# A four-layer image model on one core: eight PSUM banks for the first front, and a planner that lays parts of a front side by side

## The chip, the cores and the metric

The kernel runs on one core of a Trainium2 chip. Its time is the device time of one execution in microseconds, given as the median of several runs. All data are fp32. PE is TensorE, DVE is VectorE, ACT is ScalarE, POOL is GpSimd and SP is SyncE, which issues most DMAs here.

## The reference

Eight images of 56 x 56 tokens with 192 channels go through four layers. Each layer normalizes its input in groups and adds its output to its input:

```python
x = x + _L0_conv_ref(_gn(x), ...)   # gated Toeplitz mixing along rows and columns
x = x + _L1_conv_ref(_gn(x), ...)   # shifted 7x7 window attention, 6 heads
x = x + _L2_conv_ref(_gn(x), ...)   # depthwise 3x3 convolution
x = x + _L3_conv_ref(_gn(x), ...)   # selective scan in 4 directions, 384 channels, 16 states
```

Layer 0 is `p * (o1 + o2)` with an output projection; p, q and v are `silu(x @ w.T + b)`, and o1 and o2 are Toeplitz products of q * v along the two axes. Layer 1 is softmax attention in windows of 49 tokens with a bias table and a mask. Layer 3 projects to two halves (one becomes the gate z), convolves 3x3, and then for each direction and channel runs

```python
delta = softplus(delta + delta_bias)
h[t] = exp(delta[t] * A) * h[t - 1] + delta[t] * u[t] * B[t]     # 16 states n
y[t] = sum over n of h[t] * C[t]  (+ D * u[t])
```

The four directions are summed, normalized over channels, multiplied with silu(z) and projected.

## The kernel before

**Setup.** The kernel first makes the Toeplitz coefficients, then q * v for all images (L188 to L220), then the Toeplitz products for all images (L228 to L277), then small constants.

**Front and loop.** Everything else is organized by image. `front(b)` prepares image b for the scan and consists of five stages: `gate` (the rest of layer 0), `attention` (layer 1), `conv2` (layer 2), `inner` (projection and 3x3 convolution of layer 3, for three blocks of 128 channels) and `steps` (delta, B and C, for 14 chunks). All stages carve their buffers out of one SBUF tile, `slab`. The scan itself is a loop over `pairs`: 8 images x 4 directions (`slot`) x 7 chunks of 448 tokens x 3 channel blocks `d` x 8 pairs of states `k`, that is 672 pairs for an image and 24 for a chunk. `finish(b, j)` is the end of layer 3 for one chunk.

**One pair** of the loop is, with its lines: `inject` on POOL (hs <- du, bm, L989), `decay` on ACT (two exponentials into PSUM, ps_a, L1004), `scan` on DVE (L1013), `times_c` on DVE for five of eight k and on POOL for k = 1, 4, 6 (hc, L1019), small copies of states on ACT (L994, L1026), and `add_up` on PE (eight 64-row matmuls of hc with the identity into ps_y, L1036). The tile hc has four buffers. After the eight pairs of a d, `sums` copies ps_y to SBUF on ACT (ysb, L1047, which takes one of the same four buffers), folds it on PE (L1052) and adds it to ysum on DVE (L1056, L1061). B and C of a chunk (bm, cm) are loaded by SP one chunk ahead.

**Banks.** PSUM has eight banks: ps_a takes four (two buffers of two), ps_y two and the pool `ps` two. `bank()` takes one of the two in `ps`. Fronts, `sums` and `finish` share them.

**What sets the order.** Image 0's front is drained by itself before the loop: `drain(front(0), costs.setdefault("front", []))` runs the generator to its end, and the order of its instructions on each engine is left to the framework's scheduler. This also records a cost for each engine and step, by a formula for each instruction (`Meter`); the profile puts these instructions on line L76. The loop is written in an order of its own (`manual_schedule`), and every engine executes in this order. While pair g of image b is issued, `Parts.step(limit)` may put in steps of front(b + 1), `sums` and `finish`. A generator yields `held, needs`: how many banks it now holds, and how many its next step takes. The planner keeps a model time for each engine. `fits` lets in a step if by the recorded costs it would end on ACT before a limit, on PE by 5 us after the next scan's start (`n1 + 5.0`), and on DVE without a wait over 0.2 us. A refused step gets 3 us more each time (`grace`). A part that has just taken a bank is not resumed in the same step; at most two banks are held in all. DMAs have no cost in the model, so a yield after a load says nothing of when the data will be there.

At the last chunk of an image the next front must be complete. What is left of it is then put in without a limit:

```python
if i + 1 in range(4 * NCH, len(chunks), 4 * NCH):
    while fronts[b + 1] in parts.clients:
        parts.step(anything)
```

Of the kernel before, what the change touches and what calls it, by code (L numbers as in the profile page):

```python
# [81 lines left out]
def model(ctx: ExitStack, tc: tile.TileContext, a: dict, out: bass.AP):  # L82
# [197 lines left out]
    with (  # L280
# [3 lines left out]
        tc.tile_pool(name="ps_a", bufs=2, space=PSUM) as psa,  # L284
        tc.tile_pool(name="ps_y", bufs=1, space=PSUM) as psy,
        tc.tile_pool(name="ps", bufs=2, space=PSUM) as ps,
# [82 lines left out]

        st = wp.tile([CP, 2, NCH, 6], F32, name="gn_st")  # L370
# [49 lines left out]
        def gate(b):  # L420
# [26 lines left out]
            yield 0, 0  # L447
            yield from absorb(w_p, stats0[:, b], p_b, nb[:CP, :6], CP, 6)
            for j in range(NCH):
# [3 lines left out]
                for c in range(6):  # L453
                    yield 0, 1
                    p = bank()
                    for k in range(2):
                        nc.tensor.matmul(
                            p[:CP, :CH], w_p[:, k, c * CP : (c + 1) * CP], x[:, j % 2, k, :], start=k == 0, stop=k == 1
                        )
                    yield 1, 0  # L460
                    nc.scalar.activation(s[:, c, :], p[:CP, :CH], AF.Identity, bias=nb[:CP, c : c + 1])
                yield 0, 0
                nc.scalar.activation(s, s, AF.Silu)
                usual_functions()
                for c in range(6):
# [3 lines left out]
                    yield 0, 1  # L469
# [13 lines left out]
                for m in range(2):  # L483
# [10 lines left out]
                    nc.vector.bn_stats(out=st[:, m, j, :], in_=xm)  # L494
                nc.sync.dma_start(out=blocks(x1_d[b])[:, :, tok], in_=x[:, j % 2])
# [3 lines left out]
        def attention(b):  # L499
# [36 lines left out]
            yield 0, 0  # L536
# [15 lines left out]
            for wh in range(H // WS):  # L552
# [10 lines left out]
                for m in range(4):  # L563
# [13 lines left out]
                    )  # L577
                if wh + 1 < H // WS:
                    load_x(wh + 1)
                for q in range(4):  # L580
# [52 lines left out]
                    for g in range(2):  # L633
# [9 lines left out]
                        )  # L643
                    yield 0, 1
# [13 lines left out]
                for m in range(2):  # L658
# [12 lines left out]
                    for cd, cs in ((slice(0, W - SHIFT), slice(SHIFT, W)), (slice(W - SHIFT, W), slice(0, SHIFT))):  # L671
                        nc.vector.scalar_tensor_tensor(
                            x[:, m, :, cs], pi[:, :, cd], vb[:, m : m + 1], x[:, m, :, cs], ALU.add, ALU.add
                        )
                for i0, i1, h0 in rows(wh):
# [4 lines left out]
        def conv2(b):  # L680
# [17 lines left out]

            for j in range(NCH):
                nc.sync.dma_start(out=xo[:, j % 2], in_=blocks(x2_d[b])[:, :, j * CH : (j + 1) * CH])  # L700
                yield 0, 0
                for k in range(2):
                    nc.vector.bn_stats(out=st[:, k, j, :], in_=xo[:, j % 2, k, :])
            load_x(0)
# [49 lines left out]
        def inner(b):  # L754
# [4 lines left out]
            for d in range(ND):  # L759
# [8 lines left out]
                yield 0, 0  # L768
# [3 lines left out]
                for j in range(NCH):  # L772
                    if j + 1 < NCH:
                        load_x(j + 1)
                    for u in range(2):
                        yield 0, 1
                        p = bank()
                        for k in range(2):
                            nc.tensor.matmul(
                                p[:, :CH], w_in[:, k, u * 128 : (u + 1) * 128], x[:, j % 2, k, :], start=k == 0, stop=k == 1  # L780
                            )
                        yield 1, 0
                        if u:
                            nc.scalar.activation(zt[:, j % 2, :], p[:, :CH], AF.Identity, bias=nb[:, 1:2])
                            nc.sync.dma_start(out=zr_d[b][:, d, j * CH : (j + 1) * CH], in_=zt[:, j % 2, :])
                        else:
                            nc.scalar.activation(
                                xp[:, 8 * j + 1 : 8 * j + 9, 1 : W + 1],
                                p[:, :CH].rearrange("p (h w) -> p h w", w=W),
                                AF.Identity,  # L790
                                bias=nb[:, 0:1],
                            )
                nc.sync.dma_start(out=dg, in_=dg3_d[:, d])
                yield 0, 0
# [20 lines left out]
                for src, dst in ((xc, xc_d[0][b]), (xT, z_d[b])):  # L815
                    yield 0, 0
# [13 lines left out]
        def steps(b):  # L830
# [10 lines left out]
            yield 0, 0  # L841
            for n, (o, j) in enumerate(todo):
# [10 lines left out]
                for d in range(ND):  # L853
                    yield 0, 2
                    held = []
                    for s in range(2):
                        row = slice(32 * s, 32 * s + R)
                        held.append(bank())
                        nc.tensor.matmul(
                            held[s][:, :CH], w_dt[row, o, d * 128 : (d + 1) * 128], rc[row, n % 2, :], start=True, stop=True  # L860
                        )
                    yield 2, 0
                    for s in range(2):
                        nc.scalar.activation(
                            dl[:, s, d, :], held[s][:, :CH], AF.Identity, bias=dt_b[:, 2 * o + s, d : d + 1]
                        )
                yield 0, 0
# [196 lines left out]
        class Parts:  # L1064
# [4 lines left out]
            def __init__(self):  # L1069
                self.clients = []  # L1070
                self.t = dict.fromkeys("PADE", 0.0)
# [5 lines left out]
            def add(self, work, name, now=False):  # L1077
                entry = Entry(work, costs.setdefault(name, []), now)
                self.clients.insert(0 if name != "front" else len(self.clients), entry)
                return entry  # L1080

            def fits(self, entry, limit):
# [5 lines left out]
                for engine, cost in entry.costs[entry.at]:  # L1088
# [5 lines left out]
            def resume(self, entry):  # L1094
                got = log_of(entry.work, entry.costs) if entry.at == len(entry.costs) else next(entry.work, None)
                at = entry.ready
                for engine, cost in entry.costs[entry.at]:
                    at = self.run(engine, cost, at)
                entry.at += 1
                if got is None:  # L1100
                    self.clients.remove(entry)
                    return
                entry.held, entry.needs = got
                entry.ready = at

            def step(self, limit):
                old = [e for e in self.clients if e.held]
                for entry in old + [e for e in self.clients if e not in old]:
                    while entry in self.clients:
                        if entry.held and entry not in old:  # L1110
# [11 lines left out]
        class Entry:  # L1122
            def __init__(self, work, costs, now):
                self.work, self.costs, self.now = work, costs, now
                self.at = self.held = self.needs = self.waits = 0
                self.ready = 0.0

        def log_of(work, log):

            nonlocal nc  # L1130
            nc, meter.log = meter, []
            got = next(work, None)
            log.append(meter.log)
# [3 lines left out]
        def drain(work, log=None):  # L1137

            while (next(work, None) if log is None else log_of(work, log)) is not None:
                pass  # L1140

        drain(front(0), costs.setdefault("front", []))
        with tc.manual_schedule():
# [29 lines left out]
            fronts = {}  # L1173
            ending, anything = None, dict.fromkeys("ADE", 1e9)
            for g, (i, d, k) in enumerate(pairs):
                b, slot, j = chunks[i]
                if i % (4 * NCH) == 0 and d == 0 and k == 0 and b + 1 < B:
                    fronts[b + 1] = parts.add(front(b + 1), "front")
                more = i + 1 < len(chunks)
# [32 lines left out]
                if k == 2 and g > NP:  # L1212
                    parts.add(sums(*((i, d - 1) if d else (i - 1, ND - 1))), "sums", now=True)
                if slot == 0 and b > 0 and ((j, d, k) == (0, 0, 5) or j + 1 < NCH and (d, k) == (2, 4)):
                    while ending in parts.clients:
                        parts.step(anything)
                    ending = parts.add(finish(b - 1, j + (d == 2)), "finish")

                n1 = max(parts.t["D"], fed[g + 1], set_[g + 1])
                n2 = n1 + (2.02 if on_pool(*pairs[min(g + 1, last)][1:]) else 3.11)  # L1220
                parts.step({"A": max(n2, fed[g + 2]) - 0.7, "E": n1 + 5.0, "D": 0.2})
# [111 lines left out]
```

## Time and profile before

| | |
|---|---|
| median of 3 runs (lowest to highest) | 23384.04 us (23373.92 to 23392.59) |
| the profiled execution's own time | 23375.31 us |
| its span in the profile | 23373.5 us |
| setup, until the first load of gate(0) is used | to 2487 us |
| front of image 0 by itself | 2487 to 3863 us |
| first scan of images 1 to 7 | 6250, 8733, 11217, 13690, 16167, 18646, 21133 us |
| last scan ends, then the end of layer 3 | 23164 us, 23373 us |
| PE, DVE, ACT, POOL busy | 17477, 16533, 13090, 16164 us |

The page gives busy times, then 40 slices of the span with busy tenths; a stretch of time can be asked for with the busy time of each engine in it; the list of waits puts the idle time ahead of an instruction down to the instruction or DMA that ended it; the timeline has single instructions in order of time. An instruction is named by its line, what it writes and what it reads (`hc<-ps_a,cm`). [...]

### The profile page before, as it was taken

How to read it: one execution, taken by the hardware profiler on the slowest of the kernel's cores; microseconds unless marked ns; L12 is line 12 of the kernel's file. 1: busy time of each engine (PE TensorE's matmuls, PEld its weight loads, DVE VectorE, ACT ScalarE, POOL GpSimd, SP SyncE). 2: the span in 40 equal slices, each digit the busy share in tenths (PEclk: the TensorE clock that was granted, in tenths of full speed). 3: DMA queues.
4: the chain of work that ended last, by engine and by line, in shares of the span. 5: the costliest groups of instructions: out<-in, count | busy, mean ns of one | idle time of the engine just before them, and what ended most of it. 6: DMA issues, size and time to landing. Idle time of an engine off the chain costs nothing. (4 is left out here: it accounts for less than half of the span.)

```text
span 23373.5 us, 251077 instructions
## 1 busy us (share of the span) xinstructions
PE 17477.1 (75%) x82852; PEld 7258.6 (31%) x82852; DVE 16533.0 (71%) x13158; ACT 13089.9 (56%) x32542; POOL 16163.7 (69%) x8500
## 2 busy tenths in 40 slices
PE   8866677778787778777877777787877787775555
PEld 4566333322232223222332233222322232222112
DVE  3211113887788868887788778877887788878996
ACT  3211224665767565756665666656675667565554
POOL 0000003887888778877888778877887788778997
PEclk9987777778787879687877887787878786877667
DMA  3487214434553455345543554345534554454432
GB/s 89 113 194 169 65 53 148 138 118 151 174 149 112 143 178 151 116 133 172 164 126 115 168 168 134 116 146 179 143 119 143 176 150 124 126 175 138 129 122 89
DMA packets 2536537, 3223.64 MB, mean 138 GB/s; under 512 B 1045261, under 2 KB 2488687, under 8 KB 2504272
## 3 DMA queue, kind: packets, MB, share of 16 engines
q1 hardware_dynamic: 2515010, 3091.32, 44.9%
q0 software_dynamic: 15520, 116.14, 1.3%
q8 instruction: 657, 10.76, 0.2%
q14 instruction: 646, 5.29, 0.1%
q10 hardware_dynamic: 4704, 0.12, 0.0%
HBM read 2631.56 MB, written 575.48 MB: 137 GB/s over the span
## 5 line engine op out<-in xcount | busy, mean ns | idle before, releaser
L989 POOL TENSOR_TENSOR hs<-du,bm 128x896 f32<-128x896 f32 x5376 | 11111.6, 2094 | 147.8 <-DVE ps_a L1013 134.5
L1013 DVE TENSOR_TENSOR_SCAN ps_a<-ps_a,hs 128x898 f32<-128x898 f32 x3360 | 6783.1, 2019 | 876.6 <-ACT ps_a L1004 704.9
L1036 PE MATMUL ps_y<-hc,ident_sb 64*64 64x448 f32 x43008 | 6628.7, 714 | 924.9 <-POOL hc L1019 901.5
L1004 ACT ACTIVATE ps_a<-delta,A_logs_sb 128x449 f32<-128x449 f32 x10752 | 6859.6, 638 | 348.8 <-DVE hs L1013 67.7
L1019 POOL TENSOR_TENSOR hc<-hs,cm 128x896 f32<-128x896 f32 x2016 | 4049.3, 2009 | 2961.8 <-DVE hs L1013 1613.2
L1019 DVE TENSOR_TENSOR hc<-ps_a,cm 128x896 f32<-128x896 f32 x3360 | 3668.1, 1092 | 1604.7 <-PE ps_y L1036 654.5
L1013 DVE TENSOR_TENSOR_SCAN hs<-ps_a,hs 128x898 f32<-128x898 f32 x2016 | 4066.1, 2017 | 356.9 <-ACT ps_a L1004 327.6
L1036 PEld LDWEIGHTS ps_y<-hc,ident_sb 64*64 64x64 f32 x43008 | 1466.3, 162 | 4500.0 <-issue 2667.5
L1026 ACT COPY state<-ps_a 128x2 f32<-128x2 f32 x3359 | 535.6, 159 | 3542.9 <-DVE hc L1019 3536.5
L977 POOL TENSOR_TENSOR du<-delta,xcd 128x448 f32<-128x448 f32 x672 | 712.9, 1061 | 1319.3 <-DMA xcd<-xc 1319.3
L1052 PE MATMUL ps_f<-ysb,fold 128*64 128x448 f32 x2684 | 919.1, 774 | 704.9 <-ACT ysb L1047 564.9
L800 PE MATMUL ps_f<-slab 128*128 128x448 f32 x2646 | 1153.5, 573 | 118.2 <-DMA slab<-dg_d 108.9
L263 PE MATMUL ps_tz<-tzx,tm 112*112 112x112 f32 x4608 | 889.4, 369 | 469.6 <-issue 306.1
L277 POOL DMA_DIRECT2D o<-tzx x192 | 98.0, 514 | 1496.9 <-DVE tzx L269 1010.6
L263 PEld LDWEIGHTS ps_tz<-tzx,tm 112*112 112x112 f32 x4608 | 884.0, 200 | 475.3 <-issue 474.2
L269 DVE COPY tzx<-ps_tz 112x448 f32<-112x448 f32 x288 | 179.9, 625 | 1178.4 <-PE ps_tz L263 866.9
L1047 ACT COPY ysb<-ps_y 128x896 f32<-128x896 f32 x671 | 605.0, 902 | 572.7 <-PE ps_y L1036 571.3
L1026 ACT COPY state<-hs 128x2 f32<-128x2 f32 x2016 | 381.2, 189 | 940.8 <-DVE hs L1013 908.1
L732 PE MATMUL ps_f<-slab 96*96 96x448 f32 x1764 | 785.5, 583 | 105.0 <-DVE slab L719 94.0
L76 PE MATMUL ps_f<-slab 96*96 96x448 f32 (+6 forms) x2306 | 780.8, 520 | 92.4 <-DMA slab<-x 29.2
L269 ACT COPY tzx<-ps_tz 112x448 f32<-112x448 f32 x288 | 153.3, 532 | 1204.2 <-PE ps_tz L263 947.7
L994 ACT COPY hs<-state 128x2 f32<-128x2 f32 x4608 | 817.6, 177 | 3.5 <-POOL hc L1019 3.1
(223 smaller groups left out, 19723.7 us busy)
## 6 DMA issues: line engine op xcount, KB each, us to landing
bm<-bc SPq DMA_DIRECT2D x1792, 448.0 KB
cm<-bc SPq DMA_DIRECT2D x1792, 448.0 KB
xcd<-xc SPq DMA_DIRECT2D x840, 224.0 KB
dl<-slab SPq DMA_DIRECT2D x224, 672.0 KB
delta<-dl SPq DMA_DIRECT2D x224, 672.0 KB
tzx<-qv SPq DMA_DIRECT2D x192, 588.0 KB
o<-tzx POOLq DMA_DIRECT2D x192, 588.0 KB, 16.3
slab<-x SPq DMA_DIRECT2D x224, 336.0 KB
```

The source lines that it names most:

```text
L76: return f(*args, **kw)
L263: nc.tensor.matmul(po[:, c, :], t[:, c2 + c, :], x[:, :, c1 + c2 + c], start=True, stop=True)
L732: nc.tensor.matmul(p[:CP, :CH], dg[:, k, t, :], xp[:, u, k, dy : dy + 8, dx : dx + W], start=t == 0, stop=t == 8,)
L800: nc.tensor.matmul(p[:, :CH], dg[:, t, :], xp[:, 8 * j + dy : 8 * j + dy + 8, dx : dx + W], start=t == 0, stop=t == 8,)
L989: nc.gpsimd.tensor_mul(hs[:, :, tokens(i)[0]], dus[i, d].to_broadcast([128, NG, CH]), bms[i, k])
L994: nc.scalar.copy(hss[g][:, :, tokens(i)[1]], src)
L1004: nc.scalar.activation(dA[:, n, :], deltas[i][:, d, at : at + CH + 1], AF.Exp, scale=negA[:, slot, d, c : c + 1])
L1013: nc.vector.tensor_tensor_scan(h, dA, hs, 0.0, ALU.mult, ALU.add)
L1019: (nc.gpsimd if on_pool(d, k) else nc.vector).tensor_mul(hc, h[:, :, tokens(i)[0]], cms[i, k])
L1026: nc.scalar.copy(states[i][:, d, NG * k : NG * k + NG], h[:, :, tokens(i)[2]])
L1036: nc.tensor.matmul(yps[i, d][64 * n : 64 * n + 64, r, :CH], ident[row, row], hcs[g][row, n, :], start=k == 0, stop=k == NP - 1,)
L1052: nc.tensor.matmul(pf[64 * r : 64 * r + 64, :CH], fold, sb[:, r, :], start=True, stop=True)
```

## The change

**Banks for image 0.** The three PSUM pools are no longer opened at the top. `front(0)` is drained with a pool `ps` of eight banks, and the loop's pools (ps_a, ps_y, ps with two) are opened after it.

**Parts side by side.** A generator may now yield a list of generators. Each becomes an `Entry` of its own whose parent waits until all are done; `later` keeps their steps in the order of the list. In the front these are the six gates, the six gated products and the two outputs of `gate`, the four queries, two transposes and two outputs of `attention`, the 14 projections of `inner`, and the six deltas of `steps`. The latter took two banks at a time before and now take one each. `drain` runs up to six of a list in turn. In `gated` and `projected` the load of the next block moves behind the yield, into the step that fills the bank.

**Transfer times.** A yield may carry a third number, which is added to the time at which the planner takes the next step's inputs to be ready: 6 us after a stage's first loads, 5 before Silu in `inner`, 8 in `steps`. In `conv2` the statistics now load two blocks ahead, with a step for each `bn_stats`.

**Pace and limits.** `parts.work` sums the costs of the front's steps. `parts.late` is set while that share is behind the share of the image's pairs plus 24. While it is set, a part that has just taken a bank may go on in the same step. The limit on PE is 1.5 us in place of 5 for k = 0 and 1. `sums` gets the time at which its last add ends as its ready time.

```diff
-        tc.tile_pool(name="ps_a", bufs=2, space=PSUM) as psa,
-        tc.tile_pool(name="ps_y", bufs=1, space=PSUM) as psy,
-        tc.tile_pool(name="ps", bufs=2, space=PSUM) as ps,
...
             load_x(0)
             load_ot(0)
-            yield 0, 0
+            yield 0, 0, 6.0
...
-                for c in range(6):
+
+                def gates(c):
                     yield 0, 1
                     p = bank()
...
                     yield 1, 0
                     nc.scalar.activation(s[:, c, :], p[:CP, :CH], AF.Identity, bias=nb[:CP, c : c + 1])
-                yield 0, 0
+
+                yield [gates(c) for c in range(6)]
                 nc.scalar.activation(s, s, AF.Silu)
                 usual_functions()
-                for c in range(6):
+
+                def gated(c):
+                    yield 0, 1
                     n = 3 * j + c // 2
                     if c % 2 == 0 and n + 1 < 3 * NCH:
                         load_ot(n + 1)
-                    yield 0, 1
...
+                yield [gated(c) for c in range(6)]
+                yield [output(m) for m in range(2)]
...
+            def load_all(j):
+                nc.sync.dma_start(out=xo[:, j % 2], in_=blocks(x2_d[b])[:, :, j * CH : (j + 1) * CH])
+
+            load_all(0)
+            load_all(1)
+            yield 0, 0, 6.0
             for j in range(NCH):
-                nc.sync.dma_start(out=xo[:, j % 2], in_=blocks(x2_d[b])[:, :, j * CH : (j + 1) * CH])
-                yield 0, 0
                 for k in range(2):
                     nc.vector.bn_stats(out=st[:, k, j, :], in_=xo[:, j % 2, k, :])
+                    yield 0, 0, 2.0
+                if j + 2 < NCH:
+                    load_all(j + 2)
...
+                yield [projected(j, u) for j in range(NCH) for u in range(2)]
                 nc.sync.dma_start(out=dg, in_=dg3_d[:, d])
-                yield 0, 0
+                yield 0, 0, 6.0
...
-                    yield 0, 0
+                    yield 0, 0, 5.0
                     nc.scalar.activation(src, src, AF.Silu)
...
             load_x(0)
-            yield 0, 0
+            yield 0, 0, 8.0
...
+                def delta_of(d, s):
+                    yield 0, 1
+                    row = slice(32 * s, 32 * s + R)
+                    p = bank()
+                    nc.tensor.matmul(
+                        p[:, :CH], w_dt[row, o, d * 128 : (d + 1) * 128], rc[row, n % 2, :], start=True, stop=True
+                    )
+                    yield 1, 0
+                    nc.scalar.activation(dl[:, s, d, :], p[:, :CH], AF.Identity, bias=dt_b[:, 2 * o + s, d : d + 1])
+
+                yield [delta_of(d, s) for d in range(ND) for s in range(2)]
...
             def resume(self, entry):
-                got = log_of(entry.work, entry.costs) if entry.at == len(entry.costs) else next(entry.work, None)
+                if entry.at == len(entry.costs):
+                    entry.costs.append(([], []))
+                    got = log_of(entry.work, entry.costs[-1][0])
+                else:
+                    got = next(entry.work, None)
                 at = entry.ready
-                for engine, cost in entry.costs[entry.at]:
+                log, logs = entry.costs[entry.at]
+                for engine, cost in log:
                     at = self.run(engine, cost, at)
+                    if entry.front:
+                        self.work += cost
                 entry.at += 1
+                entry.held = entry.needs = 0
+                entry.ready = at
                 if got is None:
                     self.clients.remove(entry)
-                    return
-                entry.held, entry.needs = got
-                entry.ready = at
+                    if entry.parent is not None:
+                        entry.parent.side.remove(entry)
+                        entry.parent.ready = max(entry.parent.ready, at)
+                elif isinstance(got, list):
+                    for n, work in enumerate(got):
+                        if n == len(logs):
+                            logs.append([])
+                        entry.side.append(Entry(work, logs[n], entry.now, entry))
+                    at = self.clients.index(entry)
+                    self.clients[at:at] = entry.side
+                else:
+                    entry.held, entry.needs, *load = got
+                    entry.ready += sum(load)
+
+            def later(self, entry):
+
+                if entry.side:
+                    return True
+                if entry.parent is None or entry is entry.parent.side[0]:
+                    return False
+                side = entry.parent.side
+                return side[side.index(entry) - 1].at <= entry.at
...
-                    while entry in self.clients:
-                        if entry.held and entry not in old:
+                    while entry in self.clients and not self.later(entry):
+                        if entry.held and entry not in old and not self.late:
                             break
...
-        drain(front(0), costs.setdefault("front", []))
+        with tc.tile_pool(name="ps0", bufs=8, space=PSUM) as ps:
+            drain(front(0), costs.setdefault("front", []))
+        psa = ctx.enter_context(tc.tile_pool(name="ps_a", bufs=2, space=PSUM))
+        psy = ctx.enter_context(tc.tile_pool(name="ps_y", bufs=1, space=PSUM))
+        ps = ctx.enter_context(tc.tile_pool(name="ps", bufs=2, space=PSUM))
...
-                    parts.add(sums(*((i, d - 1) if d else (i - 1, ND - 1))), "sums", now=True)
+                    parts.add(sums(*((i, d - 1) if d else (i - 1, ND - 1))), "sums", now=True).ready = summed[g - 3]
...
+                parts.late = parts.work * image < whole * (g % image + 24)
 
                 n1 = max(parts.t["D"], fed[g + 1], set_[g + 1])
                 n2 = n1 + (2.02 if on_pool(*pairs[min(g + 1, last)][1:]) else 3.11)
-                parts.step({"A": max(n2, fed[g + 2]) - 0.7, "E": n1 + 5.0, "D": 0.2})
+                parts.step({"A": max(n2, fed[g + 2]) - 0.7, "E": n1 + (1.5 if k < 2 else 5.0), "D": 0.2})
```

## The prediction

> **What bounds the kernel now.** I read the page first, then busy time by stretch, then who waits for whom on VectorE (DVE), then the timeline at single gaps.
>
> The page shows that no engine carries the whole span.
>
> ```profile
> span 23373.5 us, 251077 instructions
> ...
> PE   8866677778787778777877777787877787775555
> ...
> DVE  3211113887788868887788778877887788878996
> ...
> POOL 0000003887888778877888778877887788778997
> ```
>
> The first four slices are the setup, up to 2487 us. Then comes image 0's front alone, until 3863 us. From there DVE, PE and POOL run together at 7 to 8 tenths until 21133 us, where image 7's scans run with no front beside them. Three parts matter: the first front (1376 us), seven loop images with a front (17,270 us) and the last image with the tail (2240 us). The change touches the first two.
>
> For the first front, the stretches are gate, attention, statistics of conv2, conv2, inner and steps. Columns: stretch, length, busy time of PE, weight loads, DVE, ACT, POOL, clock, DMA.
>
> ```profile
> 2487.00:2705.00 218.00, 202.07 (x1043) 126.17 (x1043) 46.50 (x81) 49.70 (x60) 0.00 (x0) 0.97 0.38 93
> 2705.00:3160.00 455.00, 302.29 (x1279) 179.77 (x1280) 74.08 (x187) 191.53 (x741) 0.00 (x0) 0.56 0.05 10
> 3160.00:3200.00 40.00, 10.08 (x32) 4.57 (x30) 11.57 (x25) 7.36 (x27) 0.00 (x0) 0.50 0.41 103
> 3200.00:3325.00 125.00, 116.35 (x298) 51.71 (x298) 29.11 (x53) 10.35 (x18) 0.00 (x0) 0.92 0.20 57
> 3325.00:3620.00 295.00, 219.95 (x534) 105.87 (x534) 1.22 (x4) 70.89 (x88) 0.00 (x0) 0.85 0.31 104
> 3620.00:3863.00 243.00, 157.75 (x242) 55.08 (x240) 3.87 (x4) 99.38 (x123) 13.32 (x8) 0.57 0.48 158
> ```
>
> Gate and conv2 fill PE; attention and steps fill nothing and are chains. Those two are where banks can matter.
>
> For the loop, count the scans (L1013, one for each pair) in a stretch.
>
> ```profile
> 12050.00:12600.00 550.00, 331.37 (x166) 0.69 0.38 117
> 12680.00:13100.00 420.00, 219.66 (x111) 0.90 0.44 139
> 22000.00:23000.00 1000.00, 686.59 (x345) 0.68 0.38 123
> ```
>
> A pair takes 3.31 us beside attention (550/166), 3.78 us beside conv2 and inner, 2.90 us with no front. An image with a front takes 17,270/7 = 2467 us on average, one without 2031 us. In the seven images DVE is busy 14,027 us of 17,270, so 3243 us of it is idle. Who ended that idle time, from DVE's waits over those images:
>
> ```profile
> DVE hc L1019 <- PE ps_y L1036: 653.7, 292, 12.0
> DVE hc L1019 <- PE ps_f L1052: 636.3, 294, 8.3
> DVE ps_a L1013 <- ACT ps_a L1004: 435.3, 224, 11.7
> DVE hs L1013 <- ACT ps_a L1004: 327.6, 102, 19.9
> ...
> DVE gn_st L703 <- DMA slab<-x: 92.9, 36, 8.5
> DVE ysum L1061 <- PE ps_f L1052: 90.5, 42, 2.2
> DVE slab L401 <- DMA slab<-in_w_in_dram: 79.4, 14, 6.4
> DVE slab L401 <- DMA slab<-in_w_p_dram: 63.3, 6, 11.8
> ```
>
> The loop thus loses its time on in-order queues: work of the front sits on PE and ACT ahead of the sums, products and exponentials that the scans need. The gap at the end of an image is the plainest case; the 23.1 us from scan to scan at 16101.7 stands six times (22.2 to 23.1), near chunk 27 of images 1 to 6:
>
> ```profile
> 16103.83 1.09 DVE L1019 TENSOR_TENSOR hc<-ps_a,cm 128x896 f32<-128x896 f32 x1
> 16124.82 2.03 DVE L1013 TENSOR_TENSOR_SCAN hs<-ps_a,hs 128x898 f32<-128x898 f32 x1 [19.89 <-ACT ps_a L1004]
> ```
>
> There the loop finds the front unfinished and pushes all of it out at once.
>
> **What the Trainium skill says.** "Perfetto Trace Analysis", section Optimization Strategy, says that the same gap repeating on an engine can mean too few buffers for the next tile. The first front's attention agrees: its timeline repeats every 11.61 us, with DVE waiting 4.55 us for a score matmul. "TensorE: Matmul & The Clock Gate", section What's actually happening, says that a little-used PE runs at half clock; the stretches agree (0.97 in gate, 0.56 and 0.57 in attention and steps). "ScalarE: Activation LUTs", section What ACT_TABLE_LOAD costs, gives about 1283 ns for a load; the trace has 1283 ns, four of them in the gap above. "DMA: Bandwidth & Descriptors", section Rules for kernel authors, says to issue a DMA early and wait late; here the gate's first weights are issued at 2480.44 us and first used at 2486.57, so about 6.1 us is what must be covered.
>
> **The change part by part.**
>
> *Eight banks for image 0.* Attention: the reduce of one window pair starts at 2848.05, that of the next at 2859.66. Between them the softmax and transposes are done by 2853.6 and the last copy (oT) starts at 2854.99. Only then do scores and values get banks, so the copy of v comes at 2858.92. With free banks they are computed ahead, v follows the output matmuls at 2854.99, and 0.74 us later the reduce starts: 7.7 us in place of 11.6. I take 3.7 us x 32 window pairs = **118 us** (bounds: 0 if the scheduler keeps scores behind, 126). Steps: 243 us for 14 chunks is 17.4 each; PE is busy 157.75/14 = 11.3. At best 6.1 x 14 = 85 saved, at worst 0, since dl stays single and its store was waited for up to 6.4 us; I take 3 each, **42**. Inner has 75 us of PE idle, mostly a serial Silu and copies: **10**. Gate and conv2: 0, PE covers them. The loop's own pools open only when the front is done; before, one scan and a few products ran early, some 10 us at most off the path: 0. Sum 170 (0 to 230).
>
> *Known transfer times.* The first loads of each stage get 6 us (8 in steps, 5 before Silu) before the planner places their users, and conv2's statistics load two blocks ahead instead of queueing all seven users behind SP. On DVE this concerns 92.9 + 79.4 + 63.3 us and 21.8 for w_qkv, 257 us; the other work hides them as scans go first. I take **230** (0 to 257). PE waits for the same loads at L800 (108.9), L779 (80.5) and L849 (73.5); L779 isn't covered beyond its first block. Of 182 for the other two half reaches DVE: **91** (0 to 262).
>
> *Even pace.* When the front is less than 24 pairs ahead of its even share of the work, a bank may be taken and emptied in one step. The push at an image's end then goes: 6 x (23.1 - 3.1) = 120; some of its ACT work comes back elsewhere: **110** (0 to 120).
>
> *Limit on PE.* For k = 0 and 1 the front may fill PE to only 1.5 us past the scan's start, in place of 5. So the last adds of a block meet a short queue, ysb is copied sooner, and its hc buffer returns sooner. The waits on L1052 are 636.3 + 90.5 = 727; a third gives **242** (0 to 727). What is late next is the front itself, which the pace rule makes up with k of 2 and over.
>
> *Parts side by side.* Nothing is computed more. A list costs one step to open (86 lists in an image, by the code: 21 gate, 48 attention, 3 inner, 14 steps), but then two banks fill in one step where one did. Both banks held means that a fold (84 in an image) can find none: it waits a pair, 3.4 us, with ysb kept. If one in twenty does, 84 x 0.05 x 3.4 x 7 = **100 lost** (0 to 400, one in five). The gate's load_ot moves into the filling step and its user follows one step later instead of two; PE waited for it only 17.2 us in all; I add **20 lost** (0 to 150). Its DMAs stay in SP's order ahead of bm and cm, which are loaded about six pairs (20 us) before use, so SP has cover; without it each late bm stops POOL.
>
> *Sum.* 170 + 230 + 91 + 110 + 242 - 120 = 723. The profiled execution took 23,375.3 us (span 23,373.5, 1.8 around it): 23,375 - 723 = 22,652. It lies 9 us under the median of 23,384, which is below what counts here. I say **22,650**.
>
> **The rivals.**
>
> *Only the first front gains.* For: DVE's idle time has many owners, and a wait taken away may only uncover the next; near the image's end the "late" rule is always on, and the pace before was close to even already (attention ends at chunk 16 of 28). Against: the DMA waits and the push are plain gaps with nothing else late. 23,375 - 170 = 23,205.
>
> *The whole loop goes at attention's pace.* For: attention's 3.31 us a pair has as much DVE work of its own. Against: PE is at 85 to 93% beside conv2. 672 x 3.31 = 2224 in place of 2467, times 7 is 1700; with 170: 21,505.
>
> *Slower: ACT waits behind matmuls.* In late mode the copy out of a bank is put on ACT in the step that queues its matmul. Nothing passes a waiting instruction: behind it stand the exponentials (L1004), for which the scan waits. 363 units in an image are emptied by ACT (page groups: 42 gate, 160 attention, 63 inner, 98 steps). If each holds the scan by 0.6 us, 363 x 0.6 x 7 = 1525, against savings of 673 in the loop and 170 before it: +682, 24,057. It decides from (673 + 170)/7/363 = 0.33 us each. For: DVE already waits 763 us for L1004. Against: the planner still refuses a copy that would end after its limit on ACT.
>
> **How the numbers follow.** Forecast (22,250 to 22,950) 0.50; first front only (22,950 to 23,330) 0.18; attention's pace (under 22,250) 0.15; slower 0.14; within 0.2%, about 47 us, the least this measurement can tell from none, 0.03. Faster 0.83, same 0.03, slower 0.14. For 8 in 10, I cut some half of attention's pace and most of the slower case: 21,900 to 23,450. Each bound of an unknown cost, with the others as taken, lies inside: L1052 at its best gives 22,167, the folds at their worst 22,952.
>
> **What would show it.** The first front's attention repeating near 7.7 us and the front ending about 170 us earlier; L703 and L401 gone from DVE's waits; no 23 us gap near chunk 27; the L1052 row down by a third; L1036 and L1004 no larger. I am wrong if L1004 or L1036 grows by more than the others fall, or if the attention cycle stays at 11.6.

## The result and the profile after

The changed kernel takes 23679.64 us (median of four runs, 23662.19 to 23715.51) against 23378.98 us before (four runs on the same chip, 23358.92 to 23392.59). The ratio is 1.0131, with a 95% interval of 1.0114 to 1.0149: **slower by 301 us**, where 734 us of gain were forecast. The profiled execution took 23676.19 us, and its span is 300.6 us longer.

The page of the kernel after, the lines that answer to those shown of before:

```profile
span 23674.1 us, 251107 instructions
...
DVE  3211115887788777877788778877887778778996
...
POOL 0000005877788787878787778777787878789997
```

In the seventh slice (3551 to 4143 us) DVE and POOL are busier than before (5 tenths in place of 3), as the loop starts earlier. But the last image starts later: its first scan comes at 21426 us, against 21133. The busy time of DVE is as before (16,551 against 16,533 us, its page row). So VectorE has no more work than before; it waits more.

Two stages of the first front, each cut at the same instructions in both kernels. Attention runs from the first scaling of its weights to its last sum, `steps` from its first copy of a delta to the end of its last softplus; the columns are as in the prediction. First the kernel before:

```profile
2703.32:3175.45 472.13, 313.03 (x1312) 185.02 (x1312) 77.84 (x196) 196.97 (x764) 0.00 (x0) 0.56 0.05 12
3630.76:3877.31 246.55, 163.59 (x267) 60.04 (x268) 6.46 (x7) 106.73 (x132) 19.30 (x11) 0.56 0.47 153
```

Then the kernel after:

```profile
2680.49:3112.17 431.68, 276.86 (x1312) 157.97 (x1312) 77.13 (x196) 196.85 (x764) 0.00 (x0) 0.59 0.06 13
3555.96:3716.95 160.99, 121.16 (x242) 50.23 (x240) 0.00 (x0) 88.68 (x113) 13.30 (x8) 0.60 0.69 234
```

Attention gained 40 us and `steps` 86. The gate ends 23 us earlier, 9 of them because it starts earlier, and what lies between attention and `steps` gained 12. (The prediction's cut at 3160 us lies 15 us before attention's last sum.) The front thus ends 160 us earlier, but the loop runs on from 3722 us in place of 3863, 141 us earlier: in the kernel before, the loop's second scan ran 14 us before the front's end. The seven images with a front then take from 3722 to 21426, 17,704 us in place of 17,270: +434. The last image and the tail add 8. 434 + 8 - 141 = 301.

Where an image loses, in four stretches of its 672 pairs, taken at the starts of the scans. The lines are of image 3 and count only its scans (length of the stretch, busy time and number of the scans, clock, DMA share, GB/s). For the kernel before (L1013), chunks 0 to 6 and 7 to 15:

```profile
11217.34:11863.00 645.66, 338.03 (x168) 0.89 0.55 153
11863.00:12578.23 715.23, 432.31 (x217) 0.69 0.38 117
```

For the kernel after (L1033), chunks 0 to 6, 7 to 15, 16 to 26, and 27:

```profile
11271.91:11993.81 721.90, 337.67 (x169) 0.83 0.48 138
11993.81:12770.53 776.72, 432.71 (x216) 0.74 0.39 116
12770.53:13743.73 973.20, 527.54 (x265) 0.78 0.50 165
13743.73:13814.30 70.57, 47.76 (x24) 0.67 0.38 121
```

The same stretches as means over images 1 to 6, for all kernels of this study (us; the stretches are of the one profiled execution of each, the ratio is to the kernel before, run on the same chip):

| kernel | median us | ratio, 95% interval | ch. 0-6 | 7-15 | 16-26 | 27 | image |
|---|---|---|---|---|---|---|---|
| before | 23,379 | | 653 | 715 | 1022 | 91 | 2481 |
| after | 23,680 | 1.0131 [1.0114, 1.0149] | 721 | 775 | 976 | 70 | 2542 |
| e1_banks_only | 23,251 | 0.9944 [0.9929, 0.9959] | 655 | 715 | 1023 | 91 | 2484 |
| e2_not_late | 23,848 | 1.0198 [1.0182, 1.0213] | 681 | 690 | 940 | 264 | 2575 |
| e3_late_front | 23,356 | 0.9992 [0.9983, 1.0000] | 685 | 773 | 965 | 68 | 2490 |
| e4_limit5 | 23,595 | 1.0091 [1.0075, 1.0106] | 719 | 780 | 961 | 70 | 2530 |
| e5_front_limit5 | 23,500 | 1.0044 [1.0027, 1.0061] | 712 | 770 | 964 | 68 | 2515 |
| e6_loads_known | 23,543 | 1.0065 [1.0050, 1.0080] | 666 | 704 | 987 | 170 | 2528 |
| e7_in_sequence | 23,427 | 1.0017 [1.0010, 1.0024] | 693 | 767 | 981 | 68 | 2509 |
| e8_late_minus24 | 23,591 | 1.0086 [1.0071, 1.0101] | 685 | 711 | 1005 | 128 | 2530 |
| e9_no_load_times | 23,513 | 1.0053 [1.0038, 1.0068] | 695 | 775 | 976 | 68 | 2514 |
| e10_lists_only | 23,809 | 1.0175 [1.0158, 1.0192] | 686 | 695 | 1036 | 149 | 2566 |
| e11_late_only | 23,559 | 1.0077 [1.0062, 1.0092] | 687 | 779 | 989 | 68 | 2523 |
| e12_no_lists | 23,378 | 0.9995 [0.9986, 1.0004] | 694 | 714 | 1022 | 69 | 2499 |
| e13_sums_not_late | 23,438 | 1.0023 [1.0014, 1.0032] | 702 | 773 | 967 | 68 | 2509 |
| e14_gate_lists | 23,434 | 1.0020 [1.0012, 1.0028] | 682 | 713 | 1045 | 73 | 2513 |

After against before: the end of the image gains 46 + 21 us, as hoped, but gate and attention lose 68 + 60. Who ended DVE's idle time in the seven images of the kernel after (us in total, times, longest):

```profile
DVE ps_a L1033 <- ACT ps_a L1024: 757.1, 358, 6.3
DVE hc L1039 <- PE ps_f L1072: 402.8, 214, 8.9
DVE hc L1039 <- PE ps_y L1056: 381.3, 342, 6.5
DVE hs L1033 <- ACT ps_a L1024: 320.1, 124, 6.5
DVE ysum L1081 <- PE ps_f L1072: 272.5, 135, 6.9
DVE ysum L1076 <- DMA xcd<-xc: 264.8, 68, 8.2
...
DVE slab L483 <- PE ps_f L475: 112.6, 81, 3.3
DVE slab L495 <- PE ps_f L489: 81.9, 64, 5.8
```

The waits named in the prediction fell: products behind the adds (ps_y) by 272 us, products behind the fold by 234, first loads by 119. Others rose: scans behind exponentials from 763 to 1077, the sum behind its fold from 90 to 273 and behind its load of xcd from 98 to 265, and the front's own readers right behind their matmuls (L483 and L495 from 61 to 195). The falls come to 625 us, these rises to 798. That is 173 of the 413 us by which DVE's idle time grew (3243 us before, 3656 now); the rest lies in many smaller rows, the largest of them conv2's reader behind its matmul (L762, from 18 to 72 us).

On ACT the same thing shows: a copy out of a bank now waits for its own matmul. Two of its waits before, then the same two after:

```profile
ACT slab L461 <- PE ps_f L457: 155.4, 63, 11.7
...
ACT slab L864 <- PE ps_f L859: 88.8, 131, 1.4
```

```profile
ACT slab L885 <- PE ps_f L881: 423.3, 316, 2.4
...
ACT slab L460 <- PE ps_f L456: 337.6, 216, 8.0
```

The gate's copies waited 155 us and now wait 338; those of `steps` 89, now 423. Exponentials stand behind them on ACT.

### The profile page after: what moved, and what is told of

It is laid out like the page before. It is cut to its first block, busy times and chain, and to the rows that moved or that the text cites. A ratio compares the mean times of both kernels' runs of the same rounds, so it can differ in the third digit from the quotient of the medians.

```text
span 23674.1 us, 251107 instructions
## 1 busy us (share of the span) xinstructions
PE 17342.6 (73%) x82852; PEld 7448.2 (31%) x82852; DVE 16551.5 (70%) x13158; ACT 13097.7 (55%) x32536; POOL 16162.7 (68%) x8500
## 5 line engine op out<-in xcount | busy, mean ns | idle before, releaser
L1009 POOL TENSOR_TENSOR hs<-du,bm 128x896 f32<-128x896 f32 x5376 | 11126.6, 2103 | 43.1 <-DVE ps_a L1033 24.0
L1033 DVE TENSOR_TENSOR_SCAN ps_a<-ps_a,hs 128x898 f32<-128x898 f32 x3360 | 6788.2, 2020 | 1283.7 <-ACT ps_a L1024 1099.5
L1056 PE MATMUL ps_y<-hc,ident_sb 64*64 64x448 f32 x43008 | 6381.9, 708 | 1093.3 <-POOL hc L1039 1056.1
L1024 ACT ACTIVATE ps_a<-delta,A_logs_sb 128x449 f32<-128x449 f32 x10752 | 6860.0, 638 | 345.3 <-DVE hs L1033 66.1
L1033 DVE TENSOR_TENSOR_SCAN hs<-ps_a,hs 128x898 f32<-128x898 f32 x2016 | 4065.9, 2017 | 337.8 <-ACT ps_a L1024 320.1
L1056 PEld LDWEIGHTS ps_y<-hc,ident_sb 64*64 64x64 f32 x43008 | 1587.7, 164 | 4797.9 <-issue 2893.3
L1072 PEld LDWEIGHTS ps_f<-ysb,fold 128*64 128x64 f32 x2680 | 164.7, 169 | 2423.1 <-ACT ysb L1067 1829.5
```

The source lines that it names most:

```text
L1009: nc.gpsimd.tensor_mul(hs[:, :, tokens(i)[0]], dus[i, d].to_broadcast([128, NG, CH]), bms[i, k])
L1024: nc.scalar.activation(dA[:, n, :], deltas[i][:, d, at : at + CH + 1], AF.Exp, scale=negA[:, slot, d, c : c + 1])
L1033: nc.vector.tensor_tensor_scan(h, dA, hs, 0.0, ALU.mult, ALU.add)
L1056: nc.tensor.matmul(yps[i, d][64 * n : 64 * n + 64, r, :CH], ident[row, row], hcs[g][row, n, :], start=k == 0, stop=k == NP - 1,)
L1072: nc.tensor.matmul(pf[64 * r : 64 * r + 64, :CH], fold, sb[:, r, :], start=True, stop=True)
```

## The experiments

Two theories ran through them. **A**: the late rule holds for every part, `sums` and `finish` too, and puts a reader on DVE or ACT right behind the fold, matmul or load of the same step; the loop waits there in order. **P**: what the front is short of is pairs; each rule that makes a step wait or adds one moves the front's end, and the rest is pushed out in chunk 27. No kernel leaves out work. e10, e11 and e14 are made from the kernel after: beside what their names say, they keep its ready time for `sums` and its later `load_ot`, which e1 does not have. No run takes these two by themselves.

**e1_banks_only**: before, with only the first front's banks changed.

```diff
-        drain(front(0), costs.setdefault("front", []))
+        with tc.tile_pool(name="ps0", bufs=8, space=PSUM) as ps:
+            drain(front(0), costs.setdefault("front", []))
```

> The kernel before with eight banks for image 0's front alone; planner, loads and limits stay. All theories: the front ends some 140 us earlier and the loop keeps its 2480 us an image, about 23,240 us. If the gain of the first front comes from the interleaved lists and not from the banks, it stays near 23,380.

Measured 23,251 us, and the loop's images are as before (2484 against 2481). The banks alone give nearly all of the first front's gain, 134 of 141 us. This is the best version of all: it beats both kernels.

**e2_not_late**: after, without the late rule.

```diff
-                parts.late = parts.work * image < whole * (g % image + 24)
```

> The changed kernel with the late rule never set. Theory A (the late rule puts the reader of a bank or a load in the same step as what it waits for, so DVE and ACT wait in order): the loop falls from 2540 to 2480 us an image or less, about 23,250 us, and DVE's waits for the fold in ysum (303 us) and for xcd (262 us) fall to about 100 each. Theory B (two banks filled at once by lists pack the front too densely, late or not): 23,620 to 23,700 us.

Measured 23,848 us, slower still and outside both ranges. DVE's waits for the fold in ysum are gone and those for xcd fell to 95 us, as A expected. From chunk 7 to 26 it is the quickest of all (690 and 940 us), but then the front isn't done. DVE's timeline at the end of image 3:

```profile
13855.80 2.03 DVE L1033 TENSOR_TENSOR_SCAN hs<-ps_a,hs 128x898 f32<-128x898 f32 x1 [192.34 <-ACT ps_a L1024]
```

The scan waits 192 us for the rest of the front, where the kernel before had 20. The attention put in beside image 3 spreads over 278 pairs in place of 243 (from its first softmax maximum to its last), and 13 of the 14 softplus of `steps` are left for this gap. So the late rule isn't only a cost: without it lists and load times make the front late. A alone doesn't hold.

**e3_late_front**: after, with the late rule for the front alone.

```diff
-                        if entry.held and entry not in old and not self.late:
+                        if entry.held and entry not in old and not (self.late and entry.front):
```

> The changed kernel with the late rule for parts of the front alone, not for sums and finish. Theory A: the waits of ysum for the fold and for xcd fall to about 100 each, some 350 us of DVE waiting less, 23,400 us if nothing takes their place. Theory B: within 60 us of 23,680 us.

Measured 23,356 us, 324 us below after: A is right for the loop's own parts. No sum waits for its fold any more, and of DVE's rows for the sums this is left:

```profile
DVE ysum L1076 <- DMA xcd<-xc: 48.6, 32, 5.9
```

In the kernel after one such case reads thus in the timeline of all engines:

```profile
11358.70 0.46 SPq L987 DMA_DIRECT2D xcd<-xc  x1
...
11362.80 0.97 PE L1072 MATMUL ps_f<-ysb,fold 128*64 128x448 f32 x4
11364.68 0.68 DVE L1076 SCALAR_TENSOR_TENSOR ysum<-xcd,Dsum,ps_f 128x448 f32<-128x448 f32 x1 [6.03 <-DMA xcd<-xc]
11365.28 2.03 DVE L1033 TENSOR_TENSOR_SCAN ps_a<-ps_a,hs 128x898 f32<-128x898 f32 x1
```

The load of xcd is issued at 11358.70; 5.98 us later the sum that reads it can start, and the scan stands behind the sum on DVE. With a pair between fold and sum most of this wait is covered. One loss stays in e3: scans behind exponentials still wait 1022 us (680 + 343, from 3863 to 21133 us), against 1077 in the kernel after and 763 in the kernel before.

**e13_sums_not_late**: after, late for all but `sums` (a flag on the entry), to share out the 324 us.

```diff
+                        if entry.held and entry not in old and not (self.late and not entry.sums):
```

> The changed kernel with the late rule for all but sums; finish keeps it. If sums alone carry the 324 us between the changed kernel and e3, 23,330 to 23,400 us. If finish (seven chunks beside each gate) carries a share, it stays above 23,450 us, with the first seven chunks of an image nearer to 720 than to 690 us.

Measured 23,438, between the two ranges: 241 of the 324 us are `sums`, the other 82 `finish`. DVE waits here behind its matmuls (these lines), against 7.2 and 0.2 us in e3:

```profile
DVE slab_f L951 <- PE ps_f L943: 102.1, 51, 10.0
DVE slab_f L916 <- PE ps_f L909: 54.2, 18, 4.7
```

**e4_limit5** and **e5_front_limit5**: PE's limit back at 5 us for all k, in after and in e3.

```diff
-                parts.step({..., "E": n1 + (1.5 if k < 2 else 5.0), "D": 0.2})
+                parts.step({..., "E": n1 + 5.0, "D": 0.2})
```

> The changed kernel with the PE limit of 5 us for all k. Theory C (the tight limit at k below 2 pushes the front's matmuls into other pairs and costs more than it gives): about 23,250 us. Theories A and B: the waits of hc on the fold grow back by some 200 us, 23,700 to 23,900 us.

> The changed kernel with the late rule for the front alone and the PE limit of 5 us for all k: both findings together. If they are separate losses, 23,356 - 85 = 23,270 us. If they are one loss seen twice (the tight limit only hurt because sums were put next to their matmuls), 23,340 to 23,380 us.

Measured 23,595 (85 below after) and 23,500 (144 above e3). Both miss what was expected: e4 lies between its two ranges, e5 above both of its. The tight limit thus costs in the full change and pays where the sums aren't late. In e4 DVE's row for products behind the fold rose from 403 to 734 us, and yet the kernel is faster: scans behind exponentials fell from 1077 to 752. In e5 that row is

```profile
DVE hc L1039 <- PE ps_f L1072: 774.9, 372, 7.5
```

against 568.5 in e3: 206 us, near the 242 of the prediction. The two findings don't add up, which the expectation for e5 had taken them to do.

**e8_late_minus24**: e5, late only when 24 pairs behind.

```diff
-                parts.late = parts.work * image < whole * (g % image + 24)
+                parts.late = parts.work * image < whole * (g % image - 24)
```

> As e5, but the late rule sets in only when the front is more than 24 pairs behind its even share, instead of less than 24 ahead. If being late is what makes a chunk slow (114 us for the first chunks against 105), the gates' chunks go back to about 105 us and it is 100 us or more faster than e5. If the front then ends late, the last chunk shows a push and the gain is lost: e5 plus 0 to 200 us.

Measured 23,591, 91 above e5. Gate and attention are quicker by 27 and 59 us an image, but chunks 16 to 27 lose 101: the front ends late, and the last chunk shows the push (128 us against 68), as the second expectation had it.

**e6_loads_known**: e1 with the transfer times and the early statistics loads alone.

```diff
+                entry.held, entry.needs, *load = got
+                entry.ready = at + sum(load)
...
-            yield 0, 0
+            yield 0, 0, 6.0
```

> The kernel before with eight banks for the first front and with the transfer times and the statistics loaded ahead, no lists, no late rule. As predicted for these loads: 23,251 - 321 = 22,930 us. Rival: the times and the 14 small steps of the statistics cost the front pairs that it has no slack for, so the push at the image's end grows by what the waits save: 23,200 to 23,400 us, with the gap near chunk 27 well above 23 us.

Measured 23,543, **292 us above e1**. The waits for loads fell as forecast (statistics from 94.8 us in e1 to 38.9, w_in from 81.3 to 37.5), but the statistics alone now take 14 pairs, and the softplus beside image 3 starts at pair 612 in place of 586. DVE's timeline near its end:

```profile
13683.06 2.03 DVE L1017 TENSOR_TENSOR_SCAN hs<-ps_a,hs 128x898 f32<-128x898 f32 x1 [90.98 <-ACT ps_a L1008]
```

The gap of about 20 us that the change was to close is 91 us. P is right in kind, though 23,543 lies above its 23,400 too.

**e9_no_load_times**: e3 without them.

> As e3 (late rule for the front alone, limit 1.5), but without transfer times and with conv2's statistics as before. Theory P (pairs of the loop are what the front is short of, and each pair that it idles is paid for by late steps): faster than 23,356 us by 50 to 200 us. Rival: the waits for the loads come back on DVE (about 100 us in the traces) and more, 23,450 to 23,600 us.

Measured 23,513, 157 above e3: with lists and the late rule the same load times gain. So theory P failed here, and the rival's range holds. Without the times DVE waits again for loads (statistics from 37.5 to 95.1 us, w_in from 37.5 to 81.4), and scans behind exponentials rise from 1022 us to 976 + 112.

**e10_lists_only**: e1 with the lists alone of the four rules (PE's limit 5, no late rule, no load times).

> The kernel before with eight banks for the first front and with the lists alone: no transfer times, no late rule, limit 5. Theory P: opening a list costs a step, most of all in attention's transposes (32 an image); attention takes some 30 pairs more than 243, the push near chunk 27 grows from 23 to some 100 us, about 23,650 us. Rival: two banks filled at once save steps, the front ends earlier and the push goes: 23,050 to 23,200 us.

Measured 23,809, **558 above e1**. Beside image 3 the gate's last Silu comes 14 pairs earlier (113), but attention takes 276 pairs, 33 more; the scan then waits 75 us in chunk 27. P is right in kind, its size was larger than expected. But the pairs weren't lost in attention alone. Its 33 are mostly made up before `steps`, whose first softplus comes at pair 592, against 586 in e1. From there a softplus comes every 8 pairs against every 6: the deltas filled two banks in one step before, and as a list they take one each. So five of the 14 softplus are left for pair 657, against two in e1. And 31 of the 82 us that an image loses stand in chunks 0 to 6, far from the push.

**e11_late_only**: e1 with the late rule for the front alone, and deltas one bank at a time, in sequence.

> The kernel before with eight banks for the first front and with the late rule for the front alone (margin of 24 pairs): no lists, no transfer times, limit 5. If the late rule only takes the push away: 23,251 - 110 = 23,140 us. Theory P's second half: the rule buys pairs with waits of DVE and ACT behind matmuls, the first chunks slow from 105 to about 115 us, and it ends at 23,250 to 23,420 us.

Measured 23,559, 308 above e1. That is above both expectations. Chunk 27 is free of the push (68 us), but chunks 0 to 15 lose 96 us an image. The deltas' order changed with it, so the 308 aren't the late rule's alone.

**e12_no_lists** and **e7_in_sequence**: e3 and e5 with the lists run one after the other; in e12 the deltas go in twos as before, in e7 singly.

```diff
-                yield [gates(c) for c in range(6)]
+                for c in range(6):
+                    yield from gates(c)
```

> As e3 (late rule for the front alone, limit 1.5, transfer times), but without lists: all parts in the order of the kernel before, deltas two at a time. If lists cost here as they do alone (plus 80 us an image), about 23,250 us or less. If the late rule makes up for a list's opening step, within 60 us of e3's 23,356 us.

> As e5, but every list of parts runs one after the other instead of side by side. If the lists fill two banks at once and so pack matmuls ahead of the loop's adds, this is faster than e5 by 50 us or more. If the lists are what lets the front keep its pace, it is slower by 50 us or more, with a push at the image's end.

Measured 23,378 (22 above e3, intervals of the ratios overlap) and 23,427 (73 below e5). Beside the late rule the lists gain nothing: with the limit of 1.5 us they are worth about zero, and with 5 us they cost 73, the first branch of e7's expectation. In e7 DVE's waits for products behind the adds and behind the fold are 433 and 726 us, against 476 and 775 in e5, and chunk 27 shows no push (68 us in both).

**e14_gate_lists**: e1 with lists for the gates and gated products alone, where they save pairs.

> The kernel before with eight banks for the first front and lists for the gates and gated products alone: no late rule, no transfer times, limit 5. Theory P: this list saves pairs where each other costs them (the gate ends some 13 pairs earlier), so the push near chunk 27 of 23 us goes, and it is faster than 23,251 us by 50 to 120 us. If two banks filled at once cost the gate's chunks what the push gives, it is within 50 us of 23,251 us.

Measured 23,434, 183 above e1: neither branch holds. Pairs were saved (the gate's last Silu comes at pair 115 in place of 127, and chunk 27 falls to 73 us), yet an image takes 2513 us. Two of DVE's waits from 3863 to 21133 us, which in e1 are 665.5 and 427.1:

```profile
DVE hc L1045 <- PE ps_y L1062: 747.1, 335, 13.9
...
DVE ps_a L1039 <- ACT ps_a L1030: 540.5, 252, 8.2
```

So P isn't the whole either: here saved pairs didn't save time. A likely reason is that two banks filled at once pack PE ahead of the loop's adds. That is read from these two rows, which grew by 195 us where the kernel lost 183, and e7 points the same way. But no run isolates it, and the ready time for `sums` and the later `load_ot`, which e14 has and e1 hasn't, are an untested rival.

## Why the prediction was wrong

The prediction had the sign wrong, and its range didn't reach the result. The step that failed in the full change is *Even pace*: the late rule, priced at 10 us, cost 324 us in `sums` and `finish`. Without that part (e3) the kernel is still 105 us behind e1, where the steps other than the banks were to gain 553; that rest is divided below as far as the runs allow. By its own steps:

*Eight banks: right in its sum, partly by luck.* 170 forecast, 141 measured (134 with e1). The terms were off both ways. Attention's cycle went from 11.61 to 10.63 us only, not 7.7: the scores stayed behind the transposes on PE (the bound of 0 that the text names), and the stage gained 40 us where 118 were taken. So the repeating gap was mostly the serial chain, not the lack of banks. `steps` gained 86 where 42 were taken (its softplus ran over 236 us, now 153), inner and what precedes it 12 where 10 were, and the gate's end came 23 us earlier where nothing was taken.

*Known transfer times: half right as a wait, wrong as a gain.* Forecast 230 on DVE; its four rows fell from 257 to 139, by 119. Forecast 91 on PE; its two rows (182) are 187. And e6 shows that this step alone costs 292 us. The prediction let the other work hide the delayed steps at no cost. It named no cover for the pairs that they use up. With lists and the late rule it gains 157 us (e9 against e3).

*Even pace: the failed step.* As a wait it was right: chunk 27 fell from 91 to 70 us in six images, 128 us, where 110 were forecast. But the price was put at "some of its ACT work comes back elsewhere", 10 us, with a bound of 0 for the whole gain. The rule lets any part fill a bank and empty it in one step, `sums` and `finish` too, and there its readers on DVE stand ahead of the loop's scans: 241 us for `sums` and 82 for `finish` (e13, e3).

*Limit on PE: one row came out as forecast, the gain did not.* The row of products behind the fold fell by 234, where the term was 242. But the term covers the sum's own rows behind the fold as well, and these took back 212 (272.5 and 30.2 against 90.5), since `sums` in late mode puts its add right behind the fold. In the full change the limit costs 85 us (e4); with late sums removed it is worth 144 us of time (e3 against e5).

*Parts side by side: wrong alone, nothing in the full change.* I costed 86 opening steps at nothing but a refused bank, 120 us in all, on the ground that two banks fill in one step where one did. e10 measures 558. Most of attention's lists hold two members, so each opening step isn't paid back (33 pairs more over 48 lists); the gate's hold six, or two for its outputs, and bring its last Silu 14 pairs forward. The ground didn't hold for the 14 lists of `steps`: their deltas filled two banks in one step before, and with the lists a chunk takes 8 pairs in place of 6 (e10). So the 558 have at least three parts, which no run separates: the pairs lost in attention, those lost in `steps`, and the slower first chunks. Beside the late rule the lists cost between nothing and 73 us (e12, e7).

*The slower rival: right in kind, not in place.* It put the price on ACT (a copy behind its matmul, with the exponentials behind). Scans behind exponentials did rise by 314 us, and most of that stays in e3. But what the removal gave back, 324 us, stood on DVE, in parts of the loop that the rival had not counted among those in late mode. The text said that L1036 or L1004 would grow by more than the others fall if it was wrong. L1036 (now L1056) fell and L1004 (now L1024) grew by half as much as the falls; the rest went into rows that the prediction had listed as small or not at all. So its own sign of being wrong did not appear.

*What the parts are worth.* Against e1, lists alone cost 558, load times 292, the late rule for the front with single deltas 308; the three together with PE's tight limit (e3) cost 105. So there is no sum of single costs; in part each makes up for another. One part of the change was given no price at all, the ready time of `sums`; every run from e2 on but e6 has it, and none shows its worth. What stays open: how the 105 us divide, whether e14's loss is PE's packing, and how much of e11's is the late rule.

## What to carry to other kernels

Where every engine runs in order, a reader issued in the same step as its matmul or load makes all that stands behind it wait (324 us here); keep one unit of other work between them, in the main loop's small parts too. Before you credit a removed wait in a stream that runs beside another, ask how many of the other's slots the removal uses, and what is left at its end. Measure each rule of a planner alone and with the others: here three that cost 292 to 558 us singly cost 105 together (with the tight limit on PE), and the one change beside them, banks for a phase that runs alone, was worth keeping by itself.

## What the runs showed of the hardware that was not expected

One load of xcd issued beside the loop's other traffic (DMA engines 0.48 busy in chunks 0 to 6 of that image) was readable 6.0 us after its issue, and the longest wait for such a load was 8.2 us. Otherwise nothing: the costliest instructions took nearly the same time in both kernels (a scan 2019 and 2020 ns, an add of ps_y 714 and 708, an inject 2094 and 2103); it is their order that differs.
